# Writing the last batch's final outputs in place instead of in a temporary buffer

## The chip, the cores and the metric

The kernel runs on one core of one Trainium2 chip. The time is the device time of one execution in microseconds (us); times of several executions are given as their median.

## The reference

The reference takes 4 batches of 1024 tokens with 128 features and applies two layers. Each layer normalises the tokens, puts them through an attention `s` and through a feed-forward gate `g`, and adds the product to its input:

```python
x = L0_attn_x
xn = _layernorm(x, axis=-1)
s = _L0_attn_ref(xn, ...)          # windowed attention over the 1024 tokens of a batch
g = _silu(_L0_ffn_ref(xn, ...))
x = x + s * g
xn = _layernorm(x, axis=-1)
s = _L1_attn_ref(xn, ...)          # attention over the 4 batches, for each of 1024 positions
g = _silu(_L1_ffn_ref(xn, ...))    # 128 -> 512 -> 512 -> 512 -> 128
x = x + s * g
return x
```

The change touches only the last line of the second layer, `x + s * g`, and of that only a part of the last batch.

## The kernel before

All arrays are float32. Three large arrays stay in SBUF throughout: `x` (the residual stream), `xn` (the normalised tokens) and `g1` (the gate of the second layer), each of 128 partitions x 4 batches x 1024 elements.

The work of the first layer and of the second feed-forward network is cut into eight units of 512 tokens (U = 512), half a batch each. The second layer's attention mixes the four batches at each position, so it is cut into eight slices of L = 128 columns, and a slice takes these columns of all four batches. The order of all steps on TensorE, VectorE (DVE), ScalarE (ACT) and GpSimd (POOL) is written out by hand in the string ORDER; each engine works in that order, and the framework places the semaphore waits. The DMA transfers to the output are all issued by SyncE (SP).

The steps at the end of ORDER that matter here are these.

- `i7` and `j7` are the last products of the second feed-forward network for the last unit, which is the second half of batch 3. `j7` is done twice, for 256 tokens each: products (L590) and then a SiLU on ScalarE into `g1` (L593).
- `*F` projects a slice's attention (L706). `*Y` is `gated_out`: it adds the output bias (L715), multiplies by the gate (L716), both on DVE, adds the residual on POOL (L717), and sends the result to `out` (L718).
- Slices 4 to 7 ("late") cover the columns of which the last unit's gate comes last. There `gated_out` writes the biased attention back to `xn` and finishes only batches 0 to 2.
- `y0` and `y1` are `last_batch(0)` and `last_batch(1)`. They finish batch 3 in columns 512 to 767 and 768 to 1023: a multiplication of `xn` by `g1` (L732), an addition of `x` (L733), both on DVE, and a transfer to `out` (L734).

The program ends with the words

```
*Y2 i7 *F0 *T6 *G7 *F3 *F6 *Y3 *T7 *Y6 i7 *F7 j7 *Y0 *Y7 j7 y0 y1
```

`t2k()` gives a temporary of 128 x 512 float32 from a pool with three buffers. A step that takes a `t2k` gets the buffer of the step that took one three takings earlier, and waits until that one's last use, the transfer to `out` in these steps, is over. At the end the takings are, in order, slices 2, 3, 6, 0 and 7, then `y0` and `y1`.

The rest of the program sits in one arm of an If (L862); behind it stand the closing waits and barriers, all on L932.

Of the kernel before, what the change touches and what calls it, by code (L numbers as in the profile page):

```python
# [12 lines left out]
ALU = mybir.AluOpType  # L13
# [4 lines left out]
B, S, D = 4, 1024, 128  # L18
# [104 lines left out]
def block_kernel(ctx: ExitStack, tc: tile.TileContext, a: dict, out: bass.AP):  # L123
    nc = tc.nc
    PE, DVE, ACT, POOL = nc.tensor, nc.vector, nc.scalar, nc.gpsimd
# [14 lines left out]
    def t2k():  # L140
        return tmp.tile([P, 512], F32, tag="t2k", name="t2k", bufs=3)
# [7 lines left out]
    g1 = main.tile([P, B, S], F32, tag="g1", name="g1")  # L149
# [34 lines left out]
    xn = main.tile([P, B, S], F32, tag="xn", name="xn")  # L184
# [103 lines left out]
    def program(exact):  # L288
# [438 lines left out]
        def last_batch(i):  # L727

            n = U // 2
            y = t2k()[:, 0:n]  # L730
            r = slice(U + i * n, U + i * n + n)
            DVE.tensor_tensor(y, xn[:, B - 1, r], g1[:, B - 1, r], ALU.mult)  # L732
            DVE.tensor_tensor(y, y, x[:, B - 1, r], ALU.add)  # L733
            nc.sync.dma_start(out=out[:, (B - 1) * S + r.start:(B - 1) * S + r.stop], in_=y)  # L734

# [103 lines left out]
        def scaled_w3():  # L839
# [10 lines left out]
            "z": second_gates, "Z": scaled_w3,  # L850
            "L": lambda i: load(*(("w1", "w2", "h1"), ("h2", "w3"), ("wa", "x"))[i]), "0": lambda n: idle(cst, P * n), 
            "y": last_batch,
            **{"*" + c: slices(c) for c in "ABbCENDGTFY"},
        }
        banks["next"] = iter(BANKS[BEGIN:])
        for word in ORDER.split():
            n = 2 if word[0] == "*" else 1
# [78 lines left out]
```

## Time and profile before

| quantity | value |
|---|---|
| median of 3 runs | 540.52 us (540.14 to 540.78) |
| the profiled execution, its own time | 540.1 us |
| its span, first to last instruction | 538.3 us |
| TensorE matmul busy | 520.2 us, 97% of the span |
| ScalarE, DVE, GpSimd busy | 369.1, 348.5, 124.2 us |
| L732, two instructions | 504 and 426 ns |
| L733, two instructions | 425 and 424 ns |
| L734 (128 KB each), landing after issue | 2.7 and 2.8 us |
| L718 (192 or 256 KB each), landing after issue | 2.1 to 4.4 us, median 2.6 |

Times are from the start of the span. An engine's busy time counts its instructions; waits, branches and the issuing of transfers are not counted. A transfer's landing is counted from its issue on SP to the last update of its semaphore.

### The profile page before, as it was taken

The numbers are of one execution on the slowest core, as the hardware profiler recorded it, in microseconds if no ns is written. First come the engines' busy times: TensorE is split into PE (matmuls) and PEld (weight loads), VectorE is DVE, ScalarE is ACT, GpSimd is POOL, SyncE is SP. The second block draws the span as 40 slices with busy tenths as digits, with TensorE's granted clock in tenths as the row PEclk, the third lists the DMA queues.
The fourth block names the chain that finished last, engine by engine and source line by source line (L and its number), as shares of the span: only waits on it lengthen the run. The fifth ranks groups of instructions, "written<-read, shape, count | busy, mean of one in ns | idle before, by whom it ended". The sixth has DMA issues, their size and how long they took to land.

```text
span 538.3 us, 10515 instructions
## 1 busy us (share of the span) xinstructions
PE 520.2 (97%) x4448; PEld 293.6 (55%) x4448; DVE 348.5 (65%) x657; ACT 369.1 (69%) x436; POOL 124.2 (23%) x149
## 2 busy tenths in 40 slices
PE   8599999999999999999999999999999999999994
PEld 4267554475465645555555674554564564455463
DVE  6899885466465443415745554665778577988993
ACT  3678673797859676694999637887995655765432
POOL 4013230110011010000020020211613253725762
PEclk9899999999999999999999999999999999999998
DMA  8925021110240011021301000000000000000103
GB/s 315 414 80 197 3 75 44 40 62 20 81 154 3 2 40 39 2 79 39 118 2 40 1 1 1 2 2 0 1 1 2 1 0 1 0 1 2 35 24 105
DMA packets 10727, 27.33 MB, mean 51 GB/s; under 512 B 1040, under 2 KB 5296, under 8 KB 9648
## 3 DMA queue, kind: packets, MB, share of 16 engines
q1 hardware_dynamic: 10240, 25.01, 13.3%
q10 hardware_dynamic: 432, 1.57, 0.8%
q8 instruction: 37, 0.61, 0.5%
q14 instruction: 18, 0.15, 0.1%
HBM read 24.48 MB, written 2.10 MB: 49 GB/s over the span
## 4 chain that ended last, share of the span: by engine, by line
PE 77%; DVE 12%; POOL 3%; ACT 3%; issue 2%; DMA 1%; DVEq 0%; POOLq 0%; ACTq 0%
PE ps_M L577 32%; PE ps_S L426 6%; PE ps_O L474 5%; PE ps_M L517 5%; PE ps_M L590 5%; PE ps_M L528 4%; PE ps_M L565 4%; PE ps_M L566 4%; PE ps_M L619 3%; DVE big L682 2%; DVE big L443 2%; PE ps_M L232 1%; DMA out<-t2k 1%; PE ps_M L273 1%; ACT big L777 1%
## 5 line engine op out<-in xcount | busy, mean ns | idle before, releaser
L577 PE MATMUL ps_M<-big,l1h 128*128 128x512 f32 x512 | 229.3, 595 | 0.9 <-ACT big L578 0.5
L577 PEld LDWEIGHTS ps_M<-big,l1h 128*128 128x128 f32 x512 | 94.9, 190 | 111.8 <-issue 105.9
L443 DVE TENSOR_TENSOR big<-ps_S,bias 128x2048 f32<-128x2048 f32 x32 | 73.2, 2287 | 32.4 <-PE ps_S L426 26.4
L578 ACT ACTIVATE big<-ps_M,vec 128x512 f32<-128x512 f32 x64 | 43.7, 687 | 60.5 <-PE ps_M L577 60.2
L777 ACT ACTIVATE big<-big 128x2048 f32<-128x2048 f32 x32 | 60.9, 1910 | 9.1 <-DVE big L443 8.8
L578 ACT ACT_TABLE_LOAD x41 | 52.6, 1283 | 7.6 <-PE ps_M L577 6.9
L538 POOL TENSOR_TENSOR g<-g,s 128x512 f32<-128x512 f32 x8 | 10.2, 1273 | 200.1 <-DVE s L508 130.7
L569 DVE SCALAR_TENSOR_TENSOR big<-ps_M,vec,t2k 128x512 f32<-128x512 f32 x32 | 24.0, 749 | 36.3 <-PE ps_M L566 19.9
L426 PE MATMUL ps_S<-qm,k 32*64 32x256 f32 (+1 forms) x768 | 37.4, 472 | 4.5 <-DVE big L443 4.3
L474 PEld LDWEIGHTS ps_O<-big,vb 128*32 128x32 f32 x2048 | 30.3, 112 | 11.1 <-issue 8.0
L568 ACT ACTIVATE t2k<-ps_M,vec 128x512 f32<-128x512 f32 x32 | 22.0, 686 | 19.4 <-PE ps_M L565 19.2
L474 PE MATMUL ps_O<-big,vb 128*32 128x64 f32 x2048 | 33.4, 223 | 1.0 <-issue 0.6
L565 PE MATMUL ps_M<-xn,l1w 128*128 128x512 f32 x64 | 33.4, 603 | 0.2
L566 PE MATMUL ps_M<-xn,l1w 128*128 128x512 f32 x64 | 32.8, 594 | 0.8 <-ACT t2k L568 0.8
L517 PE MATMUL ps_M<-xn,mw 128*128 128x512 f32 x64 | 33.3, 609 | 0.0
L528 PEld LDWEIGHTS ps_M<-mw,big 128*128 128x128 f32 x256 | 30.1, 192 | 4.1 <-issue 3.0
L590 PEld LDWEIGHTS ps_M<-l1w,big 128*128 128x128 f32 x256 | 30.2, 192 | 4.0 <-issue 3.6
L352 DVE SCALAR_TENSOR_TENSOR mw<-tw,gr,mw 128x512 f32<-128x512 f32 x42 | 31.1, 746 | 0.5
L528 PE MATMUL ps_M<-mw,big 128*128 128x128 f32 x256 | 31.1, 276 | 0.0
L590 PE MATMUL ps_M<-l1w,big 128*128 128x128 f32 x256 | 30.9, 276 | 0.0
L214 POOL TENSOR_SCALAR rstd<-mv 128x4 f32<-128x4 f32 x16 | 8.4, 527 | 97.3 <-DVE mv L212 90.8
L689 POOL TENSOR_TENSOR big<-big 128x512 f32<-128x512 f32 x16 | 22.2, 1387 | 34.5 <-DVE big L682 34.5
(164 smaller groups left out, 734.7 us busy)
## 6 DMA issues: line engine op xcount, KB each, us to landing
tw<-in_tw SPq DMA_DIRECT2D x24, 512.0 KB, 4.0
big<-in_tw SPq DMA_DIRECT2D x4, 1024.0 KB, 9.2
l1h<-in_l1h SPq DMA_DIRECT2D x2, 1024.0 KB, 8.6
bias<-in_bias ACTq DMA_DIRECT2D x1, 1024.0 KB, 8.7
x<-in_x SPq DMA_DIRECT2D x1, 1024.0 KB, 5.2
out<-t2k SPq DMA_DIRECT2D x4, 256.0 KB, 2.9
l1w<-in_l1w SPq DMA_DIRECT2D x3, 256.0 KB, 9.8
out<-t2k SPq DMA_DIRECT2D x4, 192.0 KB, 2.2
```

The lines of the kernel that those rows point to most:

```text
L352: DVE.scalar_tensor_tensor(m, more[e // 2][:, e % 2, :], gr[:, e:e + 1], base if e == 0 else m, ALU.mult, ALU.add)
L426: PE.matmul(sp[rows, j, :, q0:q0 + n], lhsT=k[r, key:key + W], rhs=qm[r, :, t * P + q0:t * P + q0 + n], start=True, stop=True,)
L443: DVE.tensor_tensor(pr, sp, bias, ALU.add)
L474: PE.matmul(op[32 * j:32 * j + 32, part, qs], lhsT=vb[:, col:col + 32], rhs=pr[:, j, g, qs], start=(odd + i + g == 0), stop=(odd + i + g = ...
L517: PE.matmul(hp, lhsT=m1[:, c * P:(c + 1) * P], rhs=xn[:, b, cx], start=True, stop=True)
L528: PE.matmul(op[:, i, :], lhsT=hid[:, c, i * P:(i + 1) * P], rhs=m2[:, c * D:(c + 1) * D], start=(c + i == 0), stop=(c + i == FC + 2))
L565: PE.matmul(p1, lhsT=wt["w1"][:, c * P:(c + 1) * P], rhs=xn[:, b, cx], start=True, stop=True)
L566: PE.matmul(p2, lhsT=wt["w2"][:, c * P:(c + 1) * P], rhs=xn[:, b, cx], start=True, stop=True)
L577: PE.matmul(hp, lhsT=wt[name][:, i, c * P:(c + 1) * P], rhs=hid[:, i, :], start=(i == 0), stop=(i == FC - 1))
L578: ACT.activation(new[:, c, :], hp, AF.Gelu, scale=v(name + "s", c))
L590: PE.matmul(op[:, k, :], lhsT=hid[:, i, at0:at0 + P], rhs=wt["w3"][:, i, :], start=(i + k == 0), stop=(i + k == FC + n - 2))
L777: ACT.activation(pr, pr, AF.Exp)
```

## The change

`last_batch` no longer takes a `t2k`. Its multiplication writes over the attention in `xn`, its addition works there too, and the transfer to `out` reads from `xn`. Shapes, engines, order and the number of instructions with data stay the same.

```diff
         def last_batch(i):
 
             n = U // 2
-            y = t2k()[:, 0:n]
             r = slice(U + i * n, U + i * n + n)
-            DVE.tensor_tensor(y, xn[:, B - 1, r], g1[:, B - 1, r], ALU.mult)
+            y = xn[:, B - 1, r]
+            DVE.tensor_tensor(y, y, g1[:, B - 1, r], ALU.mult)
             DVE.tensor_tensor(y, y, x[:, B - 1, r], ALU.add)
             nc.sync.dma_start(out=out[:, (B - 1) * S + r.start:(B - 1) * S + r.stop], in_=y)
```

## The prediction

> **What bounds the kernel now.** I read the page first: TensorE is busy 97% of the span, and the tenths fall to 4 only in the last of 40 slices. So a change after TensorE's last product can move the time only through the end of the program, and the whole argument is about the last 8 us. Next I read the chain of work that ended last, in order of time, from its end. Its columns are start us, us, what.
>
> ```profile
> 526.64 0.70 DVE t2k L716
> 527.34 0.03 POOLq L717
> 527.37 0.09 issue
> 527.46 1.28 POOL t2k L717
> 528.75 0.02 issue
> 528.76 4.38 DMA out<-t2k
> 533.14 0.03 issue
> 533.17 0.05 DVEq L732
> 533.22 0.04 issue
> 533.26 0.44 DVE t2k L732
> 533.70 0.02 issue
> 533.72 0.42 DVE t2k L733
> ```
>
> The reader is to see that the last multiply of `last_batch` (L732, at 533.26) is released by a DMA: an output transfer out of a `t2k` buffer, issued at 528.76, 4.38 us on its way. It is not released by the gate that the multiply reads. Which transfer it is follows from the source. `t2k` has three buffers, and the last four takers are, in this order, slice 0, slice 7, `last_batch(0)` and `last_batch(1)`; the fourth gets the buffer of the first. Slice 0's addition (L717) ends at 527.46 + 1.28 = 528.74 and its transfer is issued at 528.76. So `last_batch(1)` waits until slice 0's output has left the buffer.
>
> Third, the timeline of 529.5 to 534.5 (start us, us, engine, line, operation, tiles, in brackets idle before and releaser):
>
> ```profile
> 529.68 0.38 ACT L593 ACTIVATE g<-ps_M 128x256 f32<-128x256 f32 x1 [0.69 <-PE ps_M L590]
> 530.15 0.50 DVE L732 TENSOR_TENSOR t2k<-xn,g 128x256 f32<-128x256 f32 x1 [0.85 <-ACT g L593]
> 530.41 0.38 SPq L718 DMA_DIRECT2D out<-t2k  x1
> 530.69 0.42 DVE L733 TENSOR_TENSOR t2k<-t2k,x 128x256 f32<-128x256 f32 x1
> 531.14 3.37 SPq L734 DMA_DIRECT2D out<-t2k  x2
> 531.47 0.38 ACT L593 ACTIVATE g<-ps_M 128x256 f32<-128x256 f32 x1 [1.40 <-PE ps_M L590]
> 533.26 0.43 DVE L732 TENSOR_TENSOR t2k<-xn,g 128x256 f32<-128x256 f32 x1 [2.14 <-DMA out<-t2k]
> 533.72 0.42 DVE L733 TENSOR_TENSOR t2k<-t2k,x 128x256 f32<-128x256 f32 x1
> ```
>
> The first multiply follows its gate: ACT ends at 529.68 + 0.38 = 530.06, DVE starts at 530.15, 0.09 later. The second gate is done at 531.47 + 0.38 = 531.85, yet its multiply starts at 533.26, after 2.14 us in which DVE stands idle. That is the only place in the tail where a buffer, not data, ends a wait on the chain's last link.
>
> [...] 424 and 425 ns for L733, 426 for the undisturbed L732. [...] one line has unequal landings: L718's are 2.1 us at least, 2.6 median and 4.4 at most. [...] DVE's last branch starts at 533.7 and its next instruction comes at 537.0; SP's at 534.6 and 537.0.
>
> **The change part by part.**
>
> *Removed: two takings of `t2k`.* `last_batch(0)` loses the wait for slice 6's transfer. That costs nothing now: DVE sat idle 0.85 us for ACT, the later of the two. No other step gains, since no `t2k` is taken after these. `last_batch(1)` loses the wait for slice 0's transfer. What is late next is its gate: 531.85 + 0.09 (the handoff that the first multiply shows) = 531.94. DVE is free by then: L733 of the first half ends at 530.69 + 0.42 = 531.11. So the multiply starts 533.26 - 531.94 = **1.32 us** earlier.
>
> *Changed: four DVE instructions write to `xn` instead of `t2k`.* Same shape, same type. L733 already works in place on `t2k` at 424 ns, so I price the target at nothing: 4 x 0. From below: the first multiply took 504 ns beside POOL's L717 (529.38 to 530.38), the second 426 with POOL idle; at 531.94 POOL has been idle for 1.5 us, so even that 0.08 us isn't to be feared. Behind the multiply stand one addition (0.46 us from start to start, then 0.42) and SP's issue (534.17 now: the row of L734's two issues ends at 534.51, and one takes 0.35).
>
> *Changed: two transfers read `xn` instead of `t2k`.* Same 128 KB, same 128 rows of 1 KB into the same places in `out`, same order on SP. Issue: 0.35 us each. Landing now 2.7 and 2.8 us. The second is issued at 534.17 - 1.32 = 532.85, and SP is free, having issued the first from 531.14 to 531.49. New is the neighbourhood: it now starts 1.7 us behind the first half's transfer instead of 3.0, while that one (landing about 531.14 + 2.7 = 533.8) is still under way. Bounds: 2.1 us, the quickest of L718, and 4.4, the slowest; so -0.7 to +1.6 against 2.8. I take 2.8, because the first half's transfer itself ran beside two others and took 2.7.
>
> *Added waits.* The write to `xn` must come after what reads or wrote that part: the products of L706 and the bias addition L715, both done before (L715 of slice 7 ends at 528.66). Later writes to `xn` there are none. So nothing is queued behind a new wait, if dependences are kept by region. For that the trace has a sign: L220 reads the second half of batch 0 of `x` between 13.2 and 14.0 us while batch 1's load into the same array (issued at 11.4, 12.2 us to landing) is in flight.
>
> *After the landing.* 538.3 - (534.17 + 2.78) = 1.35 us of closing waits and barriers on L932. They follow the landing and move with it. DVE's way from its branch to L932 took 3.3 us and SP's 2.4, and both branches stand behind work that moves by 1.32; ACT's and TensorE's come before and don't matter.
>
> **Sum.** -1.32 (wait) + 0 (instructions) + 0 (landing) + 0 (close) = -1.32 us. Profiled execution: span 538.3 becomes 537.0, its own time 540.1 becomes 538.8. That execution stands 0.4 below the median of the three runs, 540.52, so the median becomes **539.2 us**.
>
> **Rivals.**
>
> *The gain is given back at the end* (17%). The second transfer runs closer behind the first and into the instruction fetches of the branches[...]. For it: the landing times of L718 spread over 2.3 us. Against it: SP's and DVE's branches shift by the same 1.32, and a 128 KB transfer already ran beside others in 2.7. Giving back half a microsecond makes 539.7, just inside no change.
>
> *A wait for the first half's transfer takes the place of the old one* (8%); this ends on the other side. Were `xn` guarded as a whole array, the second multiply would write an array that the first half's transfer is still reading, and wait on DVE for its landing: 531.14 + 2.7 = 533.8, plus the 0.12 that lies between the old landing (533.14) and the multiply (533.26), makes 533.96. That is 0.7 later than now: 541.2. It decides from the point where the first half's transfer lands after 533.14, that is after more than 2.0 us, which every transfer in the tail takes; with a landing as long as slice 0's 4.4 it would be +2.4, or 542.9. Behind it are queued the addition, the transfer and the close. Against it is the sign from `x` above; it shows reads beside a load, not a write beside an outgoing transfer, so I keep the rival.
>
> *The change does nothing* (3%): the wait goes but the multiply starts at about 533.2 for a cause the profile doesn't name, such as a semaphore that is still attached. 540.5.
>
> **How the numbers follow.** Forecast 72%, and the three rivals 17, 8 and 3%. What a measurement can tell from no change is about 0.2%, 1.08 us. Faster by more: 0.72, the forecast. Slower by more: half of the whole-array case (0.04), and 0.02 for a landing near the long bound in the other rivals. Within: 0.22. The forecast alone spans 538.4 (the landing 0.7 quicker) to 539.4; the range of 538.4 to 540.6 takes in the given-back and the nothing cases and leaves out the whole-array one.
>
> **What would show it.** Right: L732's second multiply starts within 0.2 us of 531.94 with ACT's L593 as its releaser; L732 and L733 read `xn<-xn,g` and `xn<-xn,x` at 424 to 430 ns; the second issue of L734 is near 532.85; the chain's last links run back through ACT and TensorE's L590. Wrong in the landing: the start is there but the transfer takes over 3.3 us, or L932's first wait of SP no longer names the transfer. Wrong altogether: the second L732 is released by a DMA `out<-xn` near 533.9.

## The result, and the profile after

The changed kernel takes 538.20 us (median of 8 runs, 537.63 to 538.77), the kernel before 539.97 us (median of 8 runs, 539.41 to 540.78). The ratio is 0.9964, with a 95% interval of 0.9956 to 0.9973. It is faster, by 0.36% (0.27 to 0.44%), or 1.5 to 2.4 us. The forecast was a gain of 1.32 us, to 539.2 us, with a range of 538.4 to 540.6. The direction is right; the gain is larger than forecast, and 538.20 us lies just below the range.

The end of the chain of work that ended last, in the kernel after (start us, us, what):

```profile
526.60 0.89 PE ps_O L706 x8
527.49 3.59 PE ps_M L590 x32
531.08 0.02 issue
531.11 0.39 ACT g L593
531.50 0.02 issue
531.52 0.44 DVE xn L732
531.96 0.02 issue
531.98 0.42 DVE xn L733
```

No transfer stands in it any more. It runs from TensorE's last products through the gate to the two DVE instructions. The timeline of the same stretch:

```profile
529.32 0.38 ACT L593 ACTIVATE g<-ps_M 128x256 f32<-128x256 f32 x1 [0.69 <-PE ps_M L590]
529.73 0.66 DVE L732 TENSOR_TENSOR xn<-xn,g 128x256 f32<-128x256 f32 x1 [0.70 <-ACT g L593]
530.43 0.42 DVE L733 TENSOR_TENSOR xn<-xn,x 128x256 f32<-128x256 f32 x1
530.91 1.86 SPq L734 DMA_DIRECT2D out<-xn  x2
531.11 0.38 ACT L593 ACTIVATE g<-ps_M 128x256 f32<-128x256 f32 x1 [1.40 <-PE ps_M L590]
531.52 0.42 DVE L732 TENSOR_TENSOR xn<-xn,g 128x256 f32<-128x256 f32 x1 [0.67 <-ACT g L593]
531.98 0.42 DVE L733 TENSOR_TENSOR xn<-xn,x 128x256 f32<-128x256 f32 x1
```

The second multiply is released by ScalarE and starts 0.42 us after its gate's start, where it was 1.79 us before. That is the predicted wait, gone. Slice 0's transfer itself is as slow as it was (issue to landing 4.38 us in both profiles); nothing waits for it any more. But the page's span fell from 538.3 to 535.8, by more than this.

Profiles of one kernel differ by a few tenths of a microsecond in when they reach the tail: the last L593 starts at 531.47 and 531.25 in two profiles of before, at 531.11 and 531.20 in two of after. So I compare from there on:

| from the start of the last L593, us | before | after |
|---|---|---|
| to the second L732 | 1.79 | 0.42 |
| to the second issue of L734 | 2.71 | 1.33 |
| from that issue to the landing | 2.77 | 2.05 |
| landing to the end of the span | 1.36 | 1.36 |
| sum: last L593 to the end | 6.84 | 4.74 |

The tail is 2.10 us shorter: 1.37 us is the wait and **0.72 us is the last transfer, which lands sooner**. The DMA view shows this transfer alone (KB, then us to landing), before from 534.2 and after from 532.43 us on:

```profile
out<-t2k SPq DMA_DIRECT2D x1, 128.0 KB, 2.8
out<-xn SPq DMA_DIRECT2D x1, 128.0 KB, 2.0
```

Before, both landings of L734 were 2.7 to 2.8 us. After, the first takes 2.6 and the second 2.0.

### The profile page after: what moved, and what is told of

It is laid out like the page before. It is cut to its first block, busy times and chain, and to the rows that moved or that the text cites. A ratio compares the mean times of both kernels' runs of the same rounds, so it can differ in the third digit from the quotient of the medians.

```text
span 535.8 us, 10513 instructions
## 1 busy us (share of the span) xinstructions
PE 520.1 (97%) x4448; PEld 293.6 (55%) x4448; DVE 348.7 (65%) x657; ACT 369.2 (69%) x436; POOL 122.8 (23%) x149
## 4 chain that ended last, share of the span: by engine, by line
PE 79%; DVE 11%; ACT 3%; POOL 3%; issue 2%; DVEq 0%; POOLq 0%; ACTq 0%
PE ps_M L577 32%; PE ps_S L426 5%; PE ps_M L590 5%; PE ps_O L474 5%; PE ps_M L517 5%; PE ps_M L528 4%; PE ps_M L565 4%; PE ps_M L566 4%; PE ps_M L619 3%; DVE big L682 2%; DVE big L443 2%; PE ps_M L273 1%; PE ps_M L232 1%; ACT big L777 1%; PE ps_M L314 1%
## 5 line engine op out<-in xcount | busy, mean ns | idle before, releaser
L590 PEld LDWEIGHTS ps_M<-l1w,big 128*128 128x128 f32 x256 | 30.2, 192 | 4.0 <-issue 3.6
L590 PE MATMUL ps_M<-l1w,big 128*128 128x128 f32 x256 | 30.9, 276 | 0.0
```

Source lines behind the costliest of these rows:

```text
L590: PE.matmul(op[:, k, :], lhsT=hid[:, i, at0:at0 + P], rhs=wt["w3"][:, i, :], start=(i + k == 0), stop=(i + k == FC + n - 2))
```

## The experiments

The open question was why the last transfer is quicker. The trace has 16 landing marks for each transfer, for the last one of the kernel before from 1.53 to 2.77 us after the issue. I take each mark for one part of the transfer; its landing is the last of them. An instruction fetch stands in the trace as a DMA packet of the kind "instruction", of 16 KB on queue q8 or of 8 KB on q14. Theory A: engines fetch instructions after their branch at the end of the If (L862), these fetches hold single parts of transfers up, and the last transfer now passes ahead of some of them. Theory B: it is quicker because it reads from `xn`. Theory C: that landing was the luck of one profile. "Tail" below is the time from the start of the last L593 to the end of the span, and "landing" that of the last transfer.

| run | edit | second L732 after its L593 | landing | tail | time, ratio to before (95% interval) |
|---|---|---|---|---|---|
| before_again | none | 1.78 | 2.73 | 6.78 | one run |
| again | the change | 0.42 | 2.07 | 4.76 | 0.9969 (0.9954 to 0.9984) |
| elsewhere | another target | 0.42 | 2.02 | 4.71 | 0.9961 (0.9947 to 0.9975) |
| first_only | first half only | 0.47 | 2.01 | 4.76 | 0.9964 (0.9952 to 0.9977) |
| late1 | after, 0.46 us later | 0.88 | 2.11 | 5.27 | one run |
| late3 | after, 1.4 us later | 1.79 | 2.49 | 6.56 | 1.0002 (0.9994 to 1.0011) |
| late7 | after, 3.2 us later | 3.63 | 2.08 | 7.98 | one run |
| noif_before | before, no branch | 0.75 | 1.73 | 4.72 | 0.9968 (0.9956 to 0.9980) |
| noif_after | after, no branch | 0.42 | 1.74 | 4.39 | 0.9964 (0.9950 to 0.9977) |
| pe_late | before, later branch on TensorE | 0.47 | 2.33 | 6.19 | 0.9993 (0.9986 to 1.0000) |

**The change again**, without an edit.

> The changed kernel once more. Theory A (the second transfer now passes ahead of the instruction fetches that follow the branches of TensorE and ScalarE, so it lands 0.7 us sooner): the start of the second L732 to the end of the span is 4.3 us again (5.05 before the change), the second landing 2.0 to 2.2 us, the time 1.8 to 2.0 us under the kernel before. Theory B (the transfer is quicker because it reads from xn): the same. Theory C (only the wait moved by 1.4 us; the quicker landing was the luck of one profile): landing near 2.8 us, time 1.4 us under before.

Landing 2.07 us, tail 4.76: the quick landing repeats, against C. The time is 2.2 us under before by the medians, 0.9 to 2.5 by the interval.

**Another target.**

```diff
-            y = t2k()[:, 0:n]
+            y = bias.rearrange("p j g q -> p (j g q)")[:, i * n:i * n + n]
```

> last_batch writes to a part of the bias array, which is dead by then, instead of to xn: no t2k taken, not in place, another source of the transfer. A: as the changed kernel, second L732 about 0.4 us after the start of its gate's L593, landing 2.0 to 2.2 us, 1.8 to 2.0 us under before. B: the wait goes, but the landing is 2.8 us and the gain 1.4 us. C: gain 1.4 us.

The transfer reads from `bias`, nothing is in place in the multiply, and the tail is the same: 0.42, 2.02, 4.71 us. B falls. Neither `xn` nor work in place is needed for the gain.

**Only the first half in place.**

```diff
-            y = t2k()[:, 0:n]
             r = slice(U + i * n, U + i * n + n)
+            y = t2k()[:, 0:n] if i else xn[:, B - 1, r]
```

> Only last_batch(0) works in xn; last_batch(1) takes a t2k as before. With one taking less, last_batch(1) gets the buffer of slice 6, whose transfer has landed by then. A: the whole gain, 1.8 to 2.0 us, landing 2.0 to 2.2 us. B: the second transfer reads t2k again, landing 2.8 us, gain 1.4 us. If in place work of the second half were what matters, no gain: second L732 released by a DMA near 533.3.

```profile
532.46 0.38 ACT L593 ACTIVATE g<-ps_M 128x256 f32<-128x256 f32 x1 [1.40 <-PE ps_M L590]
532.93 0.42 DVE L732 TENSOR_TENSOR t2k<-xn,g 128x256 f32<-128x256 f32 x1 [0.82 <-ACT g L593]
```

The second half writes to a `t2k` as in the kernel before and is nevertheless released by its gate. The half that waits is not the half that has to be edited: taking one `t2k` fewer ahead of it gives it slice 6's buffer, which is free by then. The whole gain is there (landing 2.01, tail 4.76), though the second transfer reads a `t2k` again.

**Later by steps.** In the kernel after, throwaway multiplies go ahead of the second half's own; `late1`, `late3` and `late7` have 1, 3 and 7.

```diff
             y = xn[:, B - 1, r]
+            for _ in range(3 * i):
+                DVE.tensor_tensor(wqkv[:, 0:n], y, g1[:, B - 1, r], ALU.mult)
             DVE.tensor_tensor(y, y, g1[:, B - 1, r], ALU.mult)
```

> The changed kernel with three throwaway multiplies of 0.46 us (they write to wqkv, which is dead by then) ahead of the second multiply of last_batch(1): the second transfer is issued about 1.4 us later, where the kernel before had it. A: the landing goes back to 2.7 to 2.9 us and the time to that of the kernel before, within 0.3 us: 1.4 us of delay cost 1.8 to 2.0. B: landing stays at 2.0 to 2.2 us, time 0.5 us under the kernel before. C: time as before, landing anything between 2.0 and 2.9 us.

Landing 2.49 us and the time of the kernel before: 1.37 us of delay cost 1.8 us of tail (6.56 against 4.76). The landing came out 0.2 short of what A asked, and well above B's. It fits C too, which allowed any landing here, but C had failed with the second profile of the changed kernel.

> The changed kernel with one throwaway multiply of 0.46 us ahead of the second multiply of last_batch(1). A: issue 0.46 us later, its data in the way of the fetches that follow TensorE's and ScalarE's return (0.8 us and 0.6 us after it): landing between 2.1 and 2.8 us, from the start of the last L593 to the end 5.2 to 6.0 us. Without such a cause: landing 2.05 us and 5.2.

Landing 2.11 us, tail 5.27: at the edge of A's range and 0.06 us from the other answer. This run tells nothing apart.

> Seven throwaway multiplies, 3.2 us: the second transfer is issued after the fetches of TensorE and ScalarE, with only those of VectorE and SyncE near it. A: landing back to 2.0 to 2.1 us though it is the latest of all, 8.0 us from the start of the last L593 to the end. If a transfer is the slower the later it is: landing 2.8 us or more, 8.7 us.

Landing 2.08 us though it is the latest of all. So it isn't lateness that costs. There is a window of time in which the last transfer is slow here (2.49 us in late3), and the kernel before had it there (2.77).

The parts of the last transfer point to the fetches as what makes that window. In every run, all parts but a few land within 1.74 us of the issue; call the rest late. The late parts are as many as the fetches that begin between the issue and 0.7 us after it: three of each in before, before_again and late3, one of each in after, again, elsewhere, first_only, late1 and late7, and none in the two runs without a branch that follow. Only pe_late, further down, is off: it has two late parts, and its fetches begin 0.8 and 1.4 us after the issue.

**Without the branch.** Both kernels with the If and its second arm (the arm for large scores) left out. The branch at the start of the If goes with it, so the tails say more here than the whole times.

```diff
-    with tc.If(fast > 0) as branch:
-        with tc.manual_schedule(engines=in_order):
-            program(False)
-    with branch.Else():
-        with tc.manual_schedule(engines=in_order):
-            program(True)
+    with tc.manual_schedule(engines=in_order):
+        program(False)
```

> The kernel before with the If and its second arm left out (the arm for large scores, which these inputs don't take): no branch at the end, so no instruction fetches after one. A (the fetches delay the last transfer): second L732 still 1.8 us after its gate (L593) starts, but landing 1.7 us instead of 2.8, so about 5.8 us from the start of the last L593 to the end of the span instead of 6.8. C (landing is luck, or due to the neighbouring transfers): landing 2.5 to 2.8 us, 6.6 to 6.8.

> The changed kernel with the If and its second arm left out. A: landing 1.7 us here too, 4.4 us from the start of the last L593 to the end; it is 1.4 us under the same kernel without the change, the wait alone, not 1.8 to 2.1. C: the difference of the two is 1.8 to 2.1 us, as with the If.

The last transfer lands in 1.73 and 1.74 us, as A says. But I had expected the wait of noif_before to stay, and its second L732 starts 0.75 us after its gate's L593, not 1.8. The chain of noif_before, its end, shows why:

```profile
528.62 1.28 POOL t2k L717
529.90 0.02 issue
529.91 2.57 DMA out<-t2k
532.49 0.03 issue
532.51 0.05 DVEq L732
532.56 0.04 issue
532.61 0.44 DVE t2k L732
```

It is the same wait for slice 0's transfer, but that one takes 2.57 us instead of 4.38. So the wait that the change removes is itself made in the main by what comes with the branch. Without the branch the two kernels' tails differ by 0.33 us (4.72 and 4.39) and not by the 1.4 us that I had expected; their medians differ by 0.27 us (538.17 and 537.90). That is less than the intervals, so only the traces show it. And even this rest has another origin: slice 0's transfer is issued 1.95 us before the last L593 here, against 2.71 us in the kernel before. Issued that early, with 2.57 us to landing, it would by estimate have been out of the buffer 0.14 us before the gate even began.

**Which fetch holds slice 0's transfer.** The kernel before, with eight throwaway products of 128 columns on TensorE between its last step and `y0`; nothing waits for them, but TensorE comes to its branch later. (The list of the products' PSUM banks, not shown, gets eight entries more.)

```diff
-    *Y2 i7 *F0 *T6 *G7 *F3 *F6 *Y3 *T7 *Y6 i7 *F7 j7 *Y0 *Y7 j7 y0 y1
+    *Y2 i7 *F0 *T6 *G7 *F3 *F6 *Y3 *T7 *Y6 i7 *F7 j7 *Y0 *Y7 j7 01 01 01 01 01 01 01 01 y0 y1
```

> The kernel before with eight throwaway products of 128 columns on TensorE after its last step (about 2 us, nothing waits for them), so that TensorE comes to its branch some 2 us later. Theory A, carried on (the fetch of 16 KB after TensorE's branch is what holds slice 0's transfer for 4.4 us, and so makes the wait for its t2k): slice 0 lands within 3.0 us of its issue, the second L732 starts within 0.5 us of its gate's end, as in the changed kernel, without the change. Where the total ends depends on where TensorE's later fetch falls on the last transfer: 538.0 to 540.5. Rival D (the fetch of 8 KB at the same moment, or the transfers of slice 7 and of the first half, hold it): slice 0 takes 4.2 to 4.5 us as before, the wait stays at 1.4 us, and the time is that of the kernel before or up to 1 us more.

The DMA view of the kernel before, from 528.7 to 533.2 us: the queues (kind, packets, MB, share) and, below, issues with KB each and the time to landing.

```profile
q8 instruction: 1, 0.02, 1.3%
q14 instruction: 2, 0.02, 1.2%
...
out<-t2k SPq DMA_DIRECT2D x1, 256.0 KB, 4.4
out<-t2k SPq DMA_DIRECT2D x1, 192.0 KB, 3.1
out<-t2k SPq DMA_DIRECT2D x1, 128.0 KB, 2.7
```

The same for pe_late, from 528.5 to 531.4 us, which is until slice 0's transfer has landed:

```profile
q14 instruction: 1, 0.01, 0.7%
...
out<-t2k SPq DMA_DIRECT2D x1, 256.0 KB, 2.8
out<-t2k SPq DMA_DIRECT2D x1, 192.0 KB, 2.1
out<-t2k SPq DMA_DIRECT2D x1, 128.0 KB, 1.7
```

The packet on q8 (16 KB) is gone from the window, one on q14 (8 KB) is still there, and all three transfers land 0.9 to 1.6 us sooner. In this kernel TensorE's branch starts at 532.9 instead of 529.3 and the 16 KB packet at 534.07 instead of 531.06; the 8 KB packet stays, 0.4 us ahead of the last gate's start in both (530.82 and 531.05). So the fetch that goes with TensorE's branch is what held slice 0's transfer, and rival D falls. In the kernel before, this one fetch held all three: in each, one part lands 0.9 us or more after all others, and these three land in the order of issue, at 533.14, 533.51 and 533.81. With slice 0 landed, the wait is gone without the change:

```profile
531.25 0.38 ACT L594 ACTIVATE g<-ps_M 128x256 f32<-128x256 f32 x1 [1.40 <-PE ps_M L591]
531.69 1.83 PE L274 MATMUL ps_M<-cst 128*128 128x128 f32 x14 [0.25 <-ACT g L594]
531.72 0.42 DVE L733 TENSOR_TENSOR t2k<-xn,g 128x256 f32<-128x256 f32 x1 [0.82 <-ACT g L594]
```

(The edit shifts the lines by one: L594 is the gate, L733 the multiply.) The time stays near that of before, since TensorE now returns from its branch at 536.53 us, 1.56 after the last landing (534.97), and so sets the end.

**The kernel before again**, for a second profile.

> The kernel before once more, for a second profile of it. If the fetches set both landings, they repeat, since the fetches come at fixed places of the program: slice 0 4.3 to 4.5 us, last transfer 2.4 to 2.8 us, 6.5 to 6.9 us from the start of the last L593 to the end. If they are luck: one of them off by over 0.5 us.

Slice 0 takes 4.37 us, the last transfer 2.73, the tail 6.78. Both slow landings belong to the kernel.

## Why the prediction was right or wrong

*The bound.* Right: only the end of the program mattered, and the second multiply's wait was the place.

*The wait, -1.32 us.* Right: -1.37 in the two profiles. The handoff from ScalarE came out 0.03 us after the gate's end instead of 0.09. What is late next was named rightly too, L593 and behind it L590.

*Instructions at nothing.* Right for the second half, 0.42 us each. The first half's multiply took 0.66 us instead of 0.50; the 0.67 us for which DVE still waits before the second multiply show that it had room.

*The landing at 2.8 us, 0 in the sum.* **This is the step that failed.** It measured 2.05 us, so the term is -0.72. The text took 2.8 because a 128 KB transfer "ran beside two others and took 2.7". That transfer was no yardstick: it was itself held by the fetch that held slice 0's, and in pe_late, beside the same two transfers, it takes 1.73 us. With the same two neighbours and without the 16 KB fetch it is 0.93 us quicker than before (2.66), so here the fetch mattered and not they. In the kernel before, the last transfer's data move from about 535.0 to 535.6 us. Three fetches begin just ahead of them, one of 16 KB at 534.49 and two of 8 KB at 534.75 and 534.86. Of its 16 parts, 13 land within 1.71 us of the issue and the last three at 2.45, 2.47 and 2.77. In the kernel after, the data move from 533.2 to 533.8; one fetch of 8 KB lies ahead of them (533.01), the other two begin at 533.98 and 534.39. Then one part alone is late, at 2.05.

*"ACT's and TensorE's come before and don't matter."* This sentence is where the reasoning slipped. Of the branches, DVE's and SP's move with the work by 1.4 us, but TensorE's and ScalarE's stay (TensorE's starts 2.19 us before the last L593 in the one profile and 2.20 in the other), and with them the fetches that follow (16 KB 0.7 to 0.9 us after TensorE's return, 8 KB 0.5 to 0.6 us after ScalarE's; the trace doesn't name a fetch's engine, I assign them by these times and, for TensorE, by pe_late). A transfer that moves is moved past those that don't. The prediction had written of this only as a loss, in the first rival; it was a gain. The bound for it stood in the text (-0.7).

*The close, 0.* Right: 1.36 us from the last landing to the end in both profiles. SP's next instruction follows the landing by 0.02 us or less in both, so SP's own way through the branch doesn't set the end.

*What the fetches cost.* The runs show a cost to transfers: slice 0's takes 4.38 us in the kernel before and 2.57 in noif_before, the last one 2.77 and 1.73. A wait of an engine for its own branch doesn't show in the time of the kernels before and after, where the end follows the last landing by the same 1.36 us; only in pe_late does an engine's own way through its branch set the end. One late part of 16 was enough: 15 of slice 0's 16 parts had landed 2.8 us after the issue, the last at 4.4.

*The base.* 540.52 us was the median of three runs; eight gave 539.97. Taken from there, the sum with the measured landing is 539.97 - 2.10 = 537.9, inside the spread of the runs of after. The range's lower end (538.4) thus missed for two reasons, the landing's term and 0.55 us of base; either alone would have stayed inside it (538.42 and 538.65).

*The rivals.* "Given back at the end" named the right neighbours, the fetches of the branches, and went the other way round. "A wait for the first half's transfer" did not come: the second L732 is released by ScalarE at 531.52, while the first half's transfer, issued at 530.91, lands at 533.49. So here a write to `xn` does not wait for a transfer that reads another region of it. "Does nothing" falls.

What stays open: the runs don't say on which of the 16 parts a fetch falls, or why slice 0's late part lands 1.6 us after all others when the fetch takes 1.0 us. For the last transfer no run moves one fetch alone: that three fetches make it late rests on the count of late parts and on the runs without a branch. `late1` didn't settle how sharp the edge of the slow window is.

## What to carry to other kernels

When a wait on a buffer's transfer stands in the chain, ask first why the transfer is slow, and compare its landing with its siblings'; here 4.4 us beside a median of 2.6 was the sign, and the wait was the product of an instruction fetch. Taking one buffer fewer ahead of the waiting step can free it as well as editing that step: here it then got a buffer whose transfer had landed. When work near the end of an If moves, set the fetches of all engines' branches beside it, those that move and those that stay.

## What the runs showed of the hardware

A fetch of 16 KB of instructions after TensorE's branch kept one part of a 256 KB transfer 1.6 us longer than the rest, and made the whole land at 4.4 us (before) instead of 2.8 (pe_late). The last transfer, of 128 KB, landed at 1.7 us with no fetch beside it (noif_before, noif_after), at 2.0 to 2.1 us with one late part, at 2.3 with two (pe_late), and at 2.5 to 2.8 us with three. Leaving out the If was worth as much as the change itself: 539.93 to 538.17 us in the kernel before. TensorE's branch took 4.3 us by its own row (3.6 us in pe_late, where it came 3.6 us later and set the end of the program).
